# One step less in the head and one more in the tail of a long LSTM, with the head's vector and scalar work put in another order

## The chip, the cores and the metric

One NeuronCore of a Trainium2 chip runs the whole kernel. The metric is the device time of one execution in microseconds (us), as the median over runs. Everything is float32.

## The reference

The input `x` is 32 sequences of 512 steps with 512 features. The output is `x` plus the hidden states of an LSTM that runs over it:

```python
xW = einsum('ntd,dg->ntg', x, Wx) + b          # 512 -> 4*512 gates
def step((h, c), xw_t):
    a = xw_t + h @ Wh                          # Wh: 512 x 2048
    i, f, o = sigmoid(a[:, :1536]) in thirds;  g = tanh(a[:, 1536:])
    c = f * c + i * g
    h = o * tanh(c)
out = x + (all h)                              # h starts as cond_1024, c as 0
```

The 512 steps must run one after another; `xW` needs no `h` and may be made ahead.

## The kernel before

**Plain and grouped steps.** The product `x_t @ Wx` is made in two ways. A *plain* step multiplies one step's 32 rows by all of Wx (`plain_block` in the head, `plain_part` in the tail). A *group* takes 32 steps at once (GS) as a matrix product cut in 4 x 2 x 4 blocks, which a fast scheme makes with 26 block products instead of 32 (R = 26); each of them is again made by 7 products instead of 8 (`ROW`, r = 1 to 7). The price is additions on VectorE: *U sums* of x blocks (`U_SUMS`, `make_sum`, called through `u_ahead`), *V sums* of weight blocks (`V_SUMS`, `v_sum`, once, in the head, then stored to DRAM in `vdram` and loaded row by row into `vring`), and *W sums* of finished products (`W_SUMS`, `W_OF`, `w_op`), whose results go to DRAM (`xwd`) and come back as one tile `xw` for each step (`load_xw`). In front of the U sums stand `pair_sum`s of the x blocks.

512 steps = 20 plain ones at the start (HEAD), 15 groups of 32, and 12 plain ones at the end (TAIL).

**The stream.** TensorE's matmuls of the groups form one list (`items`), emitted in *units* of which four make one of the 7 products of a block product (a *slot*). A group has 26 x 7 x 4 = 728 units. `emit_matmuls(n)` emits n units; `evacuate()` copies or adds finished results out of PSUM (ScalarE copies L643, L652, L659; VectorE adds L649, L653, L656) into buffers `cbuf`, and hands buffers out of the list `free_c`. Some slots begin from a bias difference that is copied into their bank before the first product (`seed_banks`, L620; which one by `BIAS_OF`; the differences are made by `early_seeds`, `second_seeds` and `late_seeds`).

**One step t** is: `h_part(t)`, 16 matmuls of h by Wh into the bank that already holds xW (L270); then stream units, or plain pieces (L198), in which TensorE is busy while `cell(t)` runs on ScalarE (L285 to L287, L292) and VectorE (L289 to L296) and leaves the transposed h for the next `h_part`. Every engine runs its instructions in the order in which the program lists them, so what stands in front of `cell(t)` on ScalarE or VectorE delays it.

**The head, t < 20.** Steps 0 to 4 have two plain steps each beside the `h_part` (`HEAD_PLAINS`: at t = 2 the plain steps 18 and 19) and jobs on VectorE: V sums, pair sums, the first U sums (`jobs`). Steps 5 to 19 run the first group's 728 units by `HEAD_STREAM`, steps 6 to 9 with one plain step more each in pieces. Plain results for t >= 14 are parked in DRAM (`kept`). From t = 5 on a step's units are cut in chunks: the first has 24 units (16 at t = 5) and `cell(t)` stands right behind it; each later chunk (12 units) begins with `evacuate`, pair sums, U sums for 24 units ahead and W sums, as many as a budget of VectorE time (`room["dve"]`) allows.

**The middle, 20 <= t < 468 (END),** has one `h_part` and 22 or 24 units in each step, the units one group ahead of the steps that use them.

**The tail.** When the stream ends, xW of the last 12 steps is made in 192 pieces of 128 columns (`plain_tail`): 11 at t = 468, 13 at t = 469, then five in each step (`due`). From t = 470 (SPLIT) on a step's bank is split in two halves with a cell each. The weights for the pieces are loaded again, since their buffers were used otherwise: one entry of `late_loads` at each t in `LATE` = (453, 455, 457, 463, 465, 467, 468); the last two (`last_load`, L229) bring the rows for c = 2 and c = 3. The rows of x for t = 500 to 503 are loaded at t = 457 into one half of `seeds_own` (`x_early`).

Of the kernel before, what the change touches and what calls it, by code (L numbers as in the profile page):

```python
# [12 lines left out]
P = 128  # L13
B = 32
T = 512
NJ = 4
G = 4
TC = 8
NCHUNK = T // TC
H = P // 2  # L20
W = G * P
HW = G * H

HEAD = 20
GS = 32
NG = 15
TAIL = T - HEAD - NG * GS
# [7 lines left out]
PARKED = 14  # L35
# [4 lines left out]
SPLIT = END + 2  # L40
LATE = (453, 455, 457, 463, 465, 467, 468)

FIRST = 13
HEAD_PLAINS = ((14, 15), (16, 17), (18, 19), (5, 6), (11, 12), (), (7,), (8,), (9,), (10,))
HEAD_STREAM = (0, 0, 0, 0, 0, 24, 52, 48, 56, 56, 56, 56, 56, 56, 56, 56, 48, 44, 36, 28)
HELD = 4
# [59 lines left out]
def kernel(  # L106
# [63 lines left out]
    def x_of(t):  # L170
        return xnat[:, xslot(t // TC), t % TC]

    x_early = seeds_own[:, 0].rearrange("p (t q b) -> p t q b", t=TC // 2, q=NJ)

    def x_plain(t):
        if 2 * TC <= t < HEAD:
            return xnat[:, 2, t % TC]
        return x_early[:, t % 4] if T - 12 <= t < T - TC else x_of(t)

# [51 lines left out]
    late_loads = [late_load(0, 0, 4), late_load(1, 0, 4)]  # L231
    late_loads += [lambda: nc.sync.dma_start(out=seeds_own[:, 0], in_=x[NCHUNK - 2][:, TC // 2 * P : TC * P])]
    late_loads += [late_load(2, 4, 6), late_load(3, 4, 6), lambda: last_load(2), lambda: last_load(3)]
# [22 lines left out]
    def half_of(t, i):  # L256
        if is_split(t):
            return PAIRS[t % 2][i][:, 0:HW]
        return bank_of(t)[:, i * HW : (i + 1) * HW]
# [61 lines left out]
    last_x = []  # L321
    free_u = [0, 1, 2, 3, 4, 5]
    room = {"dve": 0.0}
# [304 lines left out]
    def u_ahead(n):  # L628

        last = min((pos[0] + n - 1) // 4, len(items) - 1)  # L630
        if last >= 0:
            make_u(max(items[i][1] for i in range(max(0, last - 7), last + 1)))
# [171 lines left out]
    def flush_v():  # L804
        for f in v_stores:
            f()
        v_stores.clear()
# [11 lines left out]
    def split_seeds(of):  # L819
        for i in of:  # L820
            sub(seed_rows[i][:, HW:W], seed_rows[i][:, HW:W], seed_rows[i][:, 0:HW])
# [12 lines left out]
    def late_seeds():  # L834
        q = seed_rows
        split_seeds((1, 2))
        sub(q[3], q[1], q[4])
        sub(q[3], q[3], q[0])
        sub(q[1], q[1], q[2])
        seeds_made.extend(("b0-b3", "b3", "b0-b1+b2"))  # L840

# [26 lines left out]
    with tc.manual_schedule():  # L868
# [52 lines left out]
        jobs[2] = sums(21, 22, 23)  # L921
        jobs[3] = [lambda: pair_sum(0, (0, 1))] * 4 + [lambda: u_ahead(8)] + sums(24)
        jobs[4] = sums(25) + [lambda: u_ahead(24), early_seeds]
        raws = lambda *ids: [lambda s=s: v_raw(s) for s in ids]
        jobs[5] = raws(0, 7, 17, 24)
        jobs[6] = raws(1, 8, 15, 21)
        jobs[7] = raws(2, 3)
        jobs[8] = [second_seeds]
        jobs[10] = [late_seeds]
        ends = {  # L930
# [18 lines left out]
        for t in range(T):  # L949
# [25 lines left out]
            if t == 7:  # L975
                load_seeds(((0, 2),))
            if t + 2 == HEAD:
                load_xw(t + 2)
            if PARKED <= t + 3 < HEAD + NG * GS and t + 3 != HEAD:
                load_xw(t + 3)  # L980

            if t < HEAD_STEPS:
# [3 lines left out]
                if t > 4:  # L986
                    chunks.append(("stream", {5: 16}.get(t, 24), None))
                    left -= chunks[0][1]
                pieces = [(k, p, cs) for k, p in plain for cs in (((0, 1, 2, 3),) if t < 5 else ((0,), (1,), (2,), (3,)))]
# [11 lines left out]
                for i, (kind, m, cs) in enumerate(chunks):  # L1001
# [16 lines left out]
                    else:  # L1018
# [5 lines left out]
                        evacuate()  # L1024
                        if i == 0:
                            while wqueue and (room["dve"] > 2200 or len(free_c) < 1):
                                w_op(len(free_c) < 1)
                        else:
                            row_jobs(4)
                            u_ahead(m + 24)  # L1030
                            while wqueue and (
                                room["dve"] > (-2500 if t >= 13 and any(row_of(v[1]) == 0 for v in wqueue) else 800)
                                or len(free_c) < 2
                            ):
                                w_op(len(free_c) < 2)
                        seed_banks(m)
                        if i == 0 and t + 1 in SEEDED and t + 1 < HEAD:
                            seed_step(t + 1)
                        emit_matmuls(m)
                        room["dve"] += m * PROD / 4  # L1040
                        if i == 0:
                            cell(t)
                            if t + 1 == HEAD:
                                seed_step(t + 1)
                            room["dve"] -= 2500.0
                            while todo and not plains:
                                todo.pop(0)()
                                flush_v()
                if t >= 5:
                    load_v_ahead()  # L1050
# [11 lines left out]
            if t == HEAD_STEPS:  # L1062
                room["dve"] = max(room["dve"], -1500.0)
            wait_at_end[0] = t >= END - 2
# [86 lines left out]
```

## Time and profile before

| | before |
|---|---|
| median of 3 runs | 3091.01 us (3089.55 to 3091.67) |
| the profiled execution | 3091.39 us, span 3089.6 us |
| TensorE (PE) busy | 3064.1 us, 99% of the span |
| VectorE (DVE) busy | 2350.0 us, 76% |
| ScalarE (ACT) busy | 1473.4 us, 48% |
| GpSimd (POOL) busy | 240.4 us, 8% |
| mean granted TensorE clock | 0.999 |

PE is TensorE's matmul row, SP the queue that issues the DMAs. The span is from the first to the last instruction; 1.8 us of the execution lie around it. A line number such as L270 is a line of the kernel. The ends of matmuls are modelled: where they follow each other without a break, the start of the next one is the better mark.

### The profile page before, as it was taken

The page shows a single profiled execution, that of the slowest core. Times are in us where ns is not written, and L with a number is a line of the kernel's source. Part 1 is how long each engine was busy: PE and PEld are TensorE (multiplying, and loading weights), DVE is VectorE, ACT ScalarE, POOL GpSimd, SP SyncE. Part 2 cuts the span into 40 slices and gives each one's busy share as a digit, 9 for nine tenths or more (in the row PEclk, how much of TensorE's full clock was granted, in tenths as well). Part 3 has the DMA queues.
Part 4 walks back from the last instruction along what each step waited for, and adds up shares of the span by engine and source line. Part 5 has one row for each costly group of instructions (what it writes and reads, how often), then busy time and mean ns, then how long its engine had stood idle before and what let it go on. Part 6 is the DMA issues. An engine that isn't in the chain of part 4 may idle for free.

```text
span 3089.6 us, 108356 instructions
## 1 busy us (share of the span) xinstructions
PE 3064.1 (99%) x43600; PEld 1659.5 (54%) x43600; DVE 2350.0 (76%) x6382; ACT 1473.4 (48%) x5528; POOL 240.4 (8%) x508
## 2 busy tenths in 40 slices
PE   9899999999999999999999999999999999999998
PEld 7655555555555555555555555555555555555675
DVE  7678787787777878778787787878778787787644
ACT  2344544445454444545445454454544545444444
POOL 0000000000000000000000000000000000000110
PEclk9999999999999999999999999999999999999999
DMA  9788878787777777778778787877878777887530
GB/s 337 253 263 267 279 248 272 237 264 238 247 260 249 254 241 254 256 239 272 234 258 263 226 270 242 259 249 241 268 241 264 238 247 260 250 261 260 176 92 22
DMA packets 318454, 753.26 MB, mean 244 GB/s; under 512 B 50816, under 2 KB 101504, under 8 KB 317440
## 3 DMA queue, kind: packets, MB, share of 16 engines
q1 hardware_dynamic: 317952, 746.33, 74.3%
q8 instruction: 344, 5.64, 0.8%
q14 instruction: 158, 1.29, 0.1%
HBM read 564.46 MB, written 184.81 MB: 243 GB/s over the span
## 4 chain that ended last, share of the span: by engine, by line
PE 95%; DVE 2%; DMA 1%; ACT 0%; issue 0%; SPq 0%; DVEq 0%; ACTq 0%
PE gbank L270 53%; PE xbank L577 32%; PE bbank L577 5%; PE xbank L270 2%; PE xbank L207 1%; DMA vdram<-ubuf 0%; PE gbank L198 0%; DMA r<-in_L_cond_b_dram 0%; DVE prod L289 0%; DVE s L290 0%; DMA vdram<-xs 0%; DVE ubuf L771 0%; DMA xw<-kept 0%; DVE ht L296 0%; DVE hbuf L294 0%
## 5 line engine op out<-in xcount | busy, mean ns | idle before, releaser
L270 PE MATMUL gbank<-wh_sb,ht 128*32 128x512 f32 (+1 forms) x16288 | 1778.7, 575 | 6.1 <-DVE ht L296 4.4
L270 PEld LDWEIGHTS gbank<-wh_sb,ht 128*32 128x32 f32 x16288 | 607.7, 110 | 831.3 <-issue 702.9
L577 PE MATMUL xbank<-vring,ubuf 128*32 128x256 f32 (+1 forms) x13584 | 853.1, 369 | 5.5 <-ACT cbuf L659 2.3
L285 ACT ACTIVATE s<-gbank 128x128 f32<-128x128 f32 x976 | 274.0, 281 | 1213.2 <-PE gbank L270 1212.6
L577 PEld LDWEIGHTS xbank<-vring,ubuf 128*32 128x32 f32 x13584 | 527.7, 110 | 296.5 <-issue 135.1
L289 DVE TENSOR_TENSOR prod<-s 128x128 f32<-128x128 f32 x1024 | 293.4, 286 | 489.0 <-ACT s L286 484.6
L304 POOL TENSOR_TENSOR oc<-xnat,ht 128x128 f32<-128x128 f32 x504 | 240.2, 477 | 2811.4 <-DVE ht L296 1335.6
L292 ACT ACTIVATE tanh_c<-s 128x64 f32<-128x64 f32 x1024 | 262.4, 256 | 255.0 <-DVE s L290 252.3
L296 DVE STREAM_TRANSPOSE ht<-hbuf 128x64 f32<-128x64 f32 x1022 | 250.8, 245 | 75.8 <-DVE hbuf L294 1.6
L730 ACT COPY gbank<-xw 128x512 f32<-128x512 f32 x459 | 276.0, 601 | 3.7 <-DMA xw<-xwd 3.5
L290 DVE TENSOR_TENSOR s<-prod 128x64 f32<-128x64 f32 x1024 | 230.3, 225 | 35.2
L294 DVE TENSOR_TENSOR hbuf<-o,tanh_c 128x64 f32<-128x64 f32 x1024 | 211.3, 206 | 31.2 <-ACT tanh_c L292 30.7
L286 ACT ACTIVATE s<-gbank 128x64 f32<-128x64 f32 x976 | 226.0, 232 | 0.0
L437 DVE TENSOR_TENSOR cbuf<-cbuf 128x1024 f32<-128x1024 f32 x181 | 219.3, 1217 | 1.1
L577 PE MATMUL xbank<-vring,r 128*32 128x256 f32 (+1 forms) x3216 | 208.3, 357 | 0.0
L577 PE MATMUL xbank<-vring,xs 128*32 128x256 f32 (+1 forms) x3120 | 203.9, 358 | 0.0
L577 PE MATMUL bbank<-vring,ubuf 128*32 128x256 f32 (+1 forms) x2600 | 185.3, 343 | 3.8 <-DVE cbuf L649 3.8
L577 PEld LDWEIGHTS xbank<-vring,r 128*32 128x32 f32 x3216 | 123.1, 110 | 78.6 <-issue 45.7
L287 ACT ACTIVATE o<-gbank 128x128 f32<-128x128 f32 (+1 forms) x509 | 155.5, 305 | 0.0
L577 PEld LDWEIGHTS xbank<-vring,xs 128*32 128x32 f32 x3120 | 120.9, 111 | 59.0 <-issue 24.0
L643 ACT COPY cbuf<-xbank 128x512 f32<-128x512 f32 x222 | 129.5, 583 | 29.1 <-PE xbank L577 20.6
L577 PEld LDWEIGHTS bbank<-vring,ubuf 128*32 128x32 f32 x2600 | 101.3, 110 | 73.1 <-issue 41.0
(162 smaller groups left out, 2509.0 us busy)
## 6 DMA issues: line engine op xcount, KB each, us to landing
vring<-vdram SPq DMA_DIRECT2D x310, 896.0 KB, 5.7
xw<-xwd SPq DMA_DIRECT2D x1920, 64.0 KB, 4.3
xwd<-cbuf SPq DMA_DIRECT2D x135, 512.0 KB, 4.4
xwd<-r SPq DMA_DIRECT2D x85, 512.0 KB, 4.8
out_dram<-oc SPq DMA_DIRECT2D x255, 128.0 KB, 4.2
xnat<-in_x_dram SPq DMA_DIRECT2D x62, 512.0 KB, 6.4
xs<-in_x_grouped_dram SPq DMA_DIRECT2D x45, 512.0 KB, 4.7
vring<-vdram SPq DMA_DIRECT2D x33, 512.0 KB, 4.9
```

Source lines behind the costliest of these rows:

```text
L270: nc.tensor.matmul(dst[j * B : (j + 1) * B], state["ht"][:, k], m, start=False, stop=True, skip_group_check=True)
L285: nc.scalar.activation(s[:, u, 0:2], g[:, n_, 0:2], AF.Sigmoid)
L286: nc.scalar.activation(s[:, u, 2], g[:, n_, 3], AF.Tanh)
L289: nc.vector.tensor_mul(prod[:, u], s[:, u, 0:2], s[:, u, 2:4])
L290: add(nxt[:, u, 3], prod[:, u, 0], prod[:, u, 1])
L292: nc.scalar.activation(tanh_c[:, HALVES[u]], nxt[:, u, 3], AF.Tanh)
L294: nc.vector.tensor_mul(hbuf[:, HALVES[u]], o[:, u], tanh_c[:, HALVES[u]])
L296: nc.vector.transpose(ht[:, 2 * u : 2 * u + 2].rearrange("p q b -> p (q b)"), hbuf[:, HALVES[u]])
L304: (nc.gpsimd if t < T - 8 else nc.vector).tensor_add(oc[:, tt % 2], x_of(t), ht)
L437: op(c_of(dst), c_of(src), c_of(bb))
L577: nc.tensor.matmul(dst[j * B : (j + 1) * B, cols], left_of(gr, s, r)[:, j * B : (j + 1) * B], right_of(row, slot, RIGHT[r])[:, cols], star ...
L730: nc.scalar.copy(bank_of(t), src)
```

## The change

HEAD becomes 19 and TAIL 13: step 2 loses the plain step 19, and the head's last step goes. The 728 units of the first group then lie in steps 5 to 18, 60 of them in steps 10 to 14. In steps from t = 10 with at least 48 units (t = 10 to 16) the first chunk is cut to 12 units and `cell(t)` moves behind the second chunk of 24, and so behind that chunk's `evacuate` and `seed_banks`. The five operations of `late_seeds` become three jobs that are spread over the later chunks of step 10. In later chunks W sums come first and then U sums for 44 units ahead if more than three U buffers are free; the first U sums (`u_ahead(8)`) move from step 3 to step 4, behind V sum 24, and take other buffers (`free_u`); another `u_ahead(40)` is added at step 5. In the first group, the first `xw` tile of each eight steps is loaded two steps ahead instead of three. At the end of the head the VectorE budget may start at -2600 ns instead of -1500. With 13 tail steps END becomes 467 and SPLIT 469, while `LATE` stays; `x_early` holds a whole chunk of x in both halves of `seeds_own`.

```diff
-HEAD = 20
+HEAD = 19
...
-HEAD_PLAINS = ((14, 15), (16, 17), (18, 19), (5, 6), (11, 12), (), (7,), (8,), (9,), (10,))
-HEAD_STREAM = (0, 0, 0, 0, 0, 24, 52, 48, 56, 56, 56, 56, 56, 56, 56, 56, 48, 44, 36, 28)
+HEAD_PLAINS = ((14, 15), (16, 17), (18,), (5, 6), (11, 12), (), (7,), (8,), (9,), (10,))
+HEAD_STREAM = (0, 0, 0, 0, 0, 24, 52, 52, 56, 56, 60, 60, 60, 60, 60, 56, 52, 44, 36)
...
-    x_early = seeds_own[:, 0].rearrange("p (t q b) -> p t q b", t=TC // 2, q=NJ)
+    x_early = seeds_own.rearrange("p s c -> p (s c)").rearrange("p (t q b) -> p t q b", t=TC, q=NJ)
...
-        return x_early[:, t % 4] if T - 12 <= t < T - TC else x_of(t)
+        return x_early[:, t % TC] if T - TAIL <= t < T - TC else x_of(t)
...
-    late_loads += [lambda: nc.sync.dma_start(out=seeds_own[:, 0], in_=x[NCHUNK - 2][:, TC // 2 * P : TC * P])]
+    late_loads += [lambda: nc.sync.dma_start(out=seeds_own.rearrange("p s c -> p (s c)"), in_=x[NCHUNK - 2])]
...
-            return PAIRS[t % 2][i][:, 0:HW]
+            return PAIRS[(t - SPLIT) % 2][i][:, 0:HW]
...
-    free_u = [0, 1, 2, 3, 4, 5]
+    free_u = [2, 3, 0, 1, 4, 5]
...
     def late_seeds():
         q = seed_rows
-        split_seeds((1, 2))
-        sub(q[3], q[1], q[4])
-        sub(q[3], q[3], q[0])
-        sub(q[1], q[1], q[2])
-        seeds_made.extend(("b0-b3", "b3", "b0-b1+b2"))
+        return [
+            lambda: split_seeds((1, 2)),
+            lambda: (sub(q[3], q[1], q[4]), sub(q[3], q[3], q[0])),
+            lambda: (sub(q[1], q[1], q[2]), seeds_made.extend(("b0-b3", "b3", "b0-b1+b2"))),
+        ]
...
-        jobs[3] = [lambda: pair_sum(0, (0, 1))] * 4 + [lambda: u_ahead(8)] + sums(24)
-        jobs[4] = sums(25) + [lambda: u_ahead(24), early_seeds]
+        jobs[3] = [lambda: pair_sum(0, (0, 1))] * 4 + sums(24)
+        jobs[4] = [lambda: u_ahead(8)] + sums(25) + [early_seeds, lambda: u_ahead(24)]
...
-        jobs[5] = raws(0, 7, 17, 24)
+        jobs[5] = [lambda: u_ahead(40)] + raws(0, 7, 17, 24)
...
-        jobs[10] = [late_seeds]
+        jobs[10] = late_seeds()
...
-            if t + 2 == HEAD:
-                load_xw(t + 2)
-            if PARKED <= t + 3 < HEAD + NG * GS and t + 3 != HEAD:
-                load_xw(t + 3)
+            for d in (2, 3):
+                first_rows = HEAD <= t + d < HEAD + GS and (t + d - HEAD) % TC == 0
+                if PARKED <= t + d < HEAD + NG * GS and (d == 2) == first_rows:
+                    load_xw(t + d)
...
                 if t > 4:
-                    chunks.append(("stream", {5: 16}.get(t, 24), None))
-                    left -= chunks[0][1]
+                    late_cell = t >= 10 and left >= 48
+                    for m in (12, 24) if late_cell else (16 if t == 5 else 24,):
+                        chunks.append(("stream", m, None))
+                        left -= m
+                else:
+                    late_cell = False
...
                         evacuate()
-                        if i == 0:
+                        if i <= late_cell:
                             while wqueue and (room["dve"] > 2200 or len(free_c) < 1):
                                 w_op(len(free_c) < 1)
                         else:
...
                                 w_op(len(free_c) < 2)
+                            if len(free_u) > 3:
+                                u_ahead(m + 44)
                         seed_banks(m)
-                        if i == 0 and t + 1 in SEEDED and t + 1 < HEAD:
+                        if i == 0 and t + 1 in SEEDED and t + 1 != HEAD:
                             seed_step(t + 1)
                         emit_matmuls(m)
                         room["dve"] += m * PROD / 4
-                        if i == 0:
+                        if i == late_cell:
                             cell(t)
...
-                            while todo and not plains:
+                            while todo and not plains and t < 10:
                                 todo.pop(0)()
                                 flush_v()
+                        elif i > late_cell and not plains:
+                            for _ in range(-(-len(todo) // (len(chunks) - i))):
+                                todo.pop(0)()
...
-                room["dve"] = max(room["dve"], -1500.0)
+                room["dve"] = max(room["dve"], -2600.0)
```

## The prediction

> **What bounds the kernel now.** I read the page first, then the table of windows over single steps, then TensorE's waits, and then the timelines of VectorE and ScalarE at each wait.
>
> ```profile
> PE 3064.1 (99%) x43600; PEld 1659.5 (54%) x43600; DVE 2350.0 (76%) x6382; ACT 1473.4 (48%) x5528; POOL 240.4 (8%) x508
> ```
>
> TensorE is busy for 99% of the span. The change keeps its work: as many `h_part`s, 32 plain steps, 728 units per group. So it can only act on the other 1%, and on time at a lower clock. The windows (sum of each engine, then granted clock, DMA share, GB/s) show where these lie: step 10, steps 10 to 19, step 13, and everything from t = 468.
>
> ```profile
> 142.72:159.05 16.33, 12.52 (x151) 6.99 (x144) 10.02 (x25) 5.77 (x18) 0.46 (x1) 0.79 0.93 329
> 142.72:241.93 99.21, 91.47 (x1311) 48.73 (x1305) 75.38 (x176) 43.66 (x141) 4.82 (x9) 0.97 0.83 273
> 179.78:189.26 9.48, 9.48 (x149) 5.60 (x144) 6.66 (x17) 4.31 (x15) 0.46 (x1) 1.00 0.80 254
> 2883.59:3089.60 206.01, 195.78 (x3675) 133.64 (x3672) 101.77 (x385) 93.19 (x437) 21.90 (x37) 0.99 0.26 77
> ```
>
> TensorE's own waits (us in total, times, longest) name what it stands for:
>
> ```profile
> PE gbank L270 <- DVE ht L296: 4.4, 5, 1.2
> PE bbank L577 <- DVE cbuf L649: 3.8, 1, 3.8
> ...
> PE xbank L577 <- ACT cbuf L659: 2.3, 3, 0.9
> PE xbank L577 <- issue: 1.7, 1, 1.7
> ...
> PE gbank L270 <- DVE hbuf L294: 1.5, 1, 1.5
> PE xbank L577 <- DVE ubuf L491: 1.3, 1, 1.3
> ```
>
> **The price of a clean step.** Step 13 has 56 units and no idle time: 9.48 us. In it the first unit follows 3.44 us after its `h_part` began:
>
> ```profile
> 183.22 0.64 PE L577 MATMUL bbank<-vring,ubuf 128*32 128x256 f32 x8
> ```
>
> So `h_part` costs 3.44 and a unit (9.48 - 3.44) / 56 = 0.108 us.
>
> **Steps 10 to 19** hold ten `h_part`s and 492 units: 34.4 + 53.1 = 87.5 us clean, against 99.21. They lose 11.7. More than half of that is step 10, 6.85 over the clean 9.48:
>
> ```profile
> 149.87 0.43 DVE L821 TENSOR_TENSOR cbuf<-cbuf 128x256 f32<-128x256 f32 x1 [1.11 <-DMA cbuf<-in_L_cond_b_dram]
> ...
> 153.25 1.08 PE L577 MATMUL bbank<-vring,ubuf 128*32 128x256 f32 x8 [3.81 <-DVE cbuf L649]
> ```
>
> `late_seeds`, right behind `cell(10)`, waits until 149.87 for a DMA and then runs five operations, while the result that the next product needs (L649) stands behind it. Then the clock halves: at a mean of 0.79 over 16.33 us it was at half for 16.33 x 0.21 x 2 = 6.9 us, so from about 152.1, 2.7 us after TensorE had stopped; until 159.05 it cost half of 5.8 us. The change splits the five operations over the end of step 10, behind results that TensorE awaits; the loads are issued at the end of step 9 as now and should land 7.2 us into step 10 as now (149.87 - 142.72), before the third chunk ends (3.44 + 48 x 0.108 = 8.6). The differences are first needed for slot 12 at step 11, with a whole `h_part` for cover. I count all 6.85 as gone; without cover it is the 3.81.
>
> The rest, 4.8 us, are waits at the start of a later chunk, as here:
>
> ```profile
> 166.07 1.08 DVE L491 TENSOR_TENSOR ubuf<-ubuf 128x896 f32<-128x896 f32 x1
> ...
> 167.25 2.37 PE L577 MATMUL xbank<-vring,ubuf 128*32 128x256 f32 x40 [0.71 <-ACT cbuf L659]
> ```
>
> The view names L659, but slot 13's first product needs neither that copy nor its bank; it reads the U sum that ends at 167.15, queued behind the cell. The 1.7 at step 18 is also two U sums. Looking 44 units ahead, and having U sums of the second chunk ahead of the cell, takes these away.
>
> **Steps 4, 6 and 20.** At step 4 the cell stands behind a U sum that waits 5.16 us for a store out of its buffer; with the new buffer order and place it finds a buffer stored earlier, and the cell is early: -1.2 (the longest wait of `h_part` above). At step 6 the U sum of slot 3 comes at step 5: -1.3. Step 20 waits 1.5 for a cell behind three W sums and four pair sums; a budget of 3800 - 2600 = 1200 leaves room for one W sum at most: -1.5.
>
> ```profile
> 76.81 1.09 DVE L491 TENSOR_TENSOR ubuf<-xs 128x896 f32<-128x896 f32 x1 [5.16 <-DMA vdram<-ubuf]
> ```
>
> The waits of 0.8 at step 5 and 0.9 at step 7 stay: step 5 is cut as before, and at step 7 three free U buffers are left, not more than three, so slot 5's sum comes as late as now.
>
> **The step that moves.** The head loses one `h_part` and one plain step, 3.44 + 3.46 (60.44 - 56.98 below). In the tail the chain of waits shows a step with five pieces (36.87 to 41.40) and one without (54.66 to 59.13):
>
> ```profile
> 3036.87 3.45 PE gbank L270 x64
> 3040.32 1.08 PE xbank L207 x24
> 3041.40 3.45 PE xbank L270 x64
> ...
> 3054.66 2.40 PE gbank L270 x40
> ...
> 3059.13 2.42 PE xbank L270 x40
> ```
>
> Pieces fill time in which TensorE waits for the split cell: 4.53 with, 4.47 without. Of 192 pieces 24 are done at t = 468 and 469; the other 168 fill 33 split steps with five and one with three, and eight have none. After, it is 208 - 24 = 184: 36 with five, one with four, six with none: 3 x 4.53 - 2 x 4.47 = +4.65. Net of the move: -2.25.
>
> **What is late next, at step 2.** Without plain step 19, TensorE is free at 56.98. But `cell(2)` stands on VectorE behind four V sums, the last of which waits for a store, and the first half of h is there at 59.35:
>
> ```profile
> 56.98 3.72 PE L198 MATMUL xbank<-r,xnat 128*32 128x256 f32 x64
> 60.44 1.12 PE L270 MATMUL xbank<-wh_sb,ht 128*32 128x512 f32 x8
> ```
> ```profile
> 55.76 0.96 DVE L771 TENSOR_TENSOR xs<-r,vring 128x768 f32<-128x768 f32 x1 [1.86 <-DMA vdram<-xs]
> ...
> 59.11 0.24 DVE L296 STREAM_TRANSPOSE ht<-hbuf 128x64 f32<-128x64 f32 x1
> ```
>
> Nothing ahead of it changes, so 2.4 of the 3.46 come back: +2.4 (0.5 if that DMA wait went).
>
> **What is late next, in the tail.** END moves by a step, `LATE` does not. Before, the rows for c = 3 are issued during t = 468:
>
> ```profile
> L229 SPq DMA_DIRECT2D cbuf<-in_L_cond_Wx_dram x4: 422/426/432, 2880.3 to 2887.2; - x4
> ...
> DMA to landing us min/median/max: 4.1/4.2/4.8
> ```
>
> The last of them starts at 2887.2, 3.6 us after `h_part(468)` (2883.59), and lands 4.2 later, at 7.8. Their first use is in step 469 now. After the change, step 468 is the second step with pieces: pieces 11 to 23 of the list (counted from 0), c = 3 from piece 20, so at 3.44 + 9 x 3.46 / 16 = 5.4 us after `h_part(468)`. SP has the same queue ahead (the store of t = 467, four loads of `xw`). TensorE waits 7.8 - 5.4 = +2.4 (0 if SP gets there two microseconds sooner).
>
> **The new order in steps 10 to 16.** Now 12 units, a chunk's copies, and only then the cell. In step 13 the last half of h was done at 185.79, 2.57 after `h_part`:
>
> ```profile
> 185.54 0.25 DVE L296 STREAM_TRANSPOSE ht<-hbuf 128x64 f32<-128x64 f32 x1
> ```
> ```profile
> 143.41 0.58 ACT L643 COPY cbuf<-xbank 128x512 f32<-128x512 f32 x1 [3.28 <-DMA xwd<-cbuf]
> ```
>
> With 12 units (1.30) and about two copies (0.58 each by L643) ahead it is done 5.0 after, while TensorE has 52 to 60 units, 5.6 to 6.5 us: covered, with 0.6 to 1.5 to spare. Copies behind the cell then come only just before the third chunk needs them. No row shows this order. Nearest are the 0.7 waits, of which steps 10 to 19 have about one every second step; nine steps with nothing are 0, nine with 0.8 each 7.2. I take 3.
>
> **The sum:** -11.7 - 1.2 - 1.3 - 1.5 - 2.25 + 2.4 + 2.4 + 3.0 = -10.2. Four more units at step 7 are paid by later steps (728 in all). The profiled execution took 3091.39, 0.4 above the median, so about 3081 on the median's scale. About 0.2%, 6.2 us, is what a measurement of this kernel can tell from no change: 3084.8 to 3097.2.
>
> **Rivals.**
>
> *VectorE becomes the head's bound* (14%). Steps 10 to 18 are 9 x 3.44 + 488 x 0.108 = 83.7 us clean.
>
> ```profile
> L289 DVE TENSOR_TENSOR prod<-s 128x128 f32<-128x128 f32 x20 | 5.7, 287 | 13.4 <-ACT s L286 13.4
> ```
>
> The row groups the first operation of the cell's halves in the old ten steps: VectorE idles 13.4 us ahead of them. It works 75.38 us there, 73.5 without one cell (1.9 by the busy time of L289 to L296), which leaves 10.2 of 83.7. Nine tenths of 13.4 is 12.1: the head would be 1.9 us longer than clean by these waits alone. If nine tenths of all idle time stay, 0.9 x (99.21 - 75.38) = 21.4, it is 11.2 longer. Between them, at 8 instead of 3, stands this rival: 3086. Against it: W sums for rows needed later may move behind the head, where VectorE is less full (76% of the span).
>
> *The two new gaps halve the clock* (7%). Step 10 shows a drop about 2.7 us into a gap, and the new ones are 2.4. Each drop costs 2.9: 3081 + 5.8 = 3086.8. The Trainium skill (TensorE: Matmul & The Clock Gate, "Why this matters for your kernels") warns of gaps above about 3 us; by that rule neither gap is long enough, and the trace agrees in so far as the 1.7 gap brought no drop and the 3.8 one did.
>
> *Slower: a copy ahead of the cell waits for a buffer* (7%). The L643 row above shows the wait, 3.28 for a store out of `cbuf`, at a place where no cell stood behind it. In the new order one does: a wait of 3.28 uses up the 1.5 to spare, and a longer one makes a gap like step 10's, 6.85 with the clock. Shorter steps press on the buffers. Against 10.2 gained, two such gaps give 3094.7 and three 3101.6; from three of the seven steps on it is slower.
>
> **How the numbers follow.** 72% for the forecast, 3081. The rivals of 14% and 7% end within 0.2%, the last is slower. Faster by over 0.2%: 0.73 (with a little of the first rival's low end); within: 0.20; slower: 0.07. Low end: no new waits in steps 10 to 18 (-3), half of the two other gaps (-2.4), some of the two old waits: 3075. High end, with the first two rivals in it: 3089.
>
> **What would show it.** TensorE's waits should have no L649 of 3.8, no half clock before the kernel's end, and two new entries: `h_part(3)` for 2.4 on h, and L207 for 2 on the DMA of L229. The step from `h_part(10)` should take about 9.9. Steps 10 to 18 above 90 us, or a clock below 1 in them, would show me wrong; so would ScalarE waits on `xwd` ahead of L285.

## The result: slower by 0.4%

| | before | after |
|---|---|---|
| median | 3090.98 us (3089.55 to 3091.67, 7 runs) | 3102.95 us (3098.30 to 3107.99, 7 runs) |
| the profiled execution | 3091.39 us, span 3089.6 us | 3102.61 us, span 3100.8 us |

The ratio is 1.0038, with a 95% interval of 1.0028 to 1.0047: slower by about 12 us. 3081 was forecast, 3075 to 3089.

The page of the changed kernel has TensorE 4.0 us busier and the span 11.2 us longer:

```profile
PE 3068.1 (99%) x43640; PEld 1659.9 (54%) x43640; DVE 2351.3 (76%) x6383; ACT 1471.2 (47%) x5528; POOL 241.8 (8%) x508
```

The windows that answer to those of before: step 10, steps 10 to 18, step 13, then steps 19 to 23, and everything from t = 467.

```profile
138.62:148.53 9.91, 9.91 (x158) 7.76 (x152) 5.16 (x19) 5.07 (x16) 0.46 (x1) 1.00 0.97 336
138.62:234.27 95.65, 85.21 (x1271) 48.46 (x1265) 73.09 (x170) 41.68 (x133) 6.20 (x9) 1.00 0.75 257
171.40:184.51 13.11, 10.29 (x157) 4.89 (x153) 9.49 (x20) 4.87 (x16) 0.45 (x1) 1.00 0.97 331
234.27:273.36 39.09, 33.04 (x404) 15.58 (x400) 26.20 (x65) 14.45 (x54) 1.83 (x4) 0.91 0.86 266
2884.20:3100.80 216.60, 205.17 (x3808) 150.15 (x3808) 104.41 (x394) 95.16 (x447) 22.34 (x38) 0.99 0.26 76
```

Step 10 became clean, 9.91 us with no idle time and a full clock. But steps 10 to 18 take 95.65, 12.0 over the clean 83.7: by the starts of their `h_part`s, 2.9 are lost at step 11, 6.1 in steps 12 to 16 and 3.0 at step 18. In step 13, which lost nothing before, TensorE now stands for 2.8. The next five steps have 22, 22, 24, 22 and 22 units, in a clean state 4 x 5.81 + 6.02 = 29.26 (the step times before); they take 39.1. In the kernel before, the five steps behind the head took 31.0, at nearly the same DMA share and GB/s, so it is not that more bytes are moved there now:

```profile
241.93:272.93 31.00, 29.47 (x405) 15.13 (x401) 27.19 (x68) 14.55 (x55) 2.30 (x5) 1.00 0.84 261
```

TensorE's waits have new names:

```profile
PE gbank L270 <- DVE hbuf L294: 6.3, 3, 3.9
PE xbank L577 <- ACT xbank L620: 4.1, 2, 2.6
PE xbank L270 <- DVE ht L296: 3.7, 4, 1.4
PE xbank L577 <- DMA vring<-vdram: 2.8, 1, 2.8
PE xbank L207 <- DMA r<-in_L_cond_Wx_dram: 1.9, 1, 1.9
...
PE xbank L577 <- ACT xnat L659: 1.3, 1, 1.3
PE bbank L577 <- DVE r L649: 1.3, 1, 1.3
PE xbank L207 <- DMA cbuf<-in_L_cond_Wx_dram: 1.2, 1, 1.2
```

Four places stand behind most of them, each with rows of the changed kernel's timelines.

**Step 11.** The last of the bias differences (L839) ends at 154.1; it was queued behind four pair sums, a U sum and a W sum, and ScalarE's copy of it (L620) holds TensorE for 2.6:

```profile
153.43 0.68 DVE L839 TENSOR_TENSOR cbuf<-cbuf,r 128x512 f32<-128x512 f32 x1
...
154.20 1.11 ACT L620 COPY xbank<-cbuf 128x512 f32<-128x512 f32 x2 [5.00 <-DVE cbuf L839]
...
154.84 0.42 PE L577 MATMUL xbank<-vring,ubuf 128*32 128x256 f32 x4 [2.62 <-ACT xbank L620]
```

**Step 13.** The cell stands behind the evacuation of the second chunk and a W sum (177.02 to 178.15). What the next chunk needs (L649) stands behind the cell, and the chunk after it waits for L620, which ScalarE runs only after it has copied products that this first wait made late. TensorE waits twice:

```profile
177.02 1.22 DVE L437 TENSOR_TENSOR cbuf<-cbuf,r 128x1024 f32<-128x1024 f32 x1
178.15 0.28 DVE L289 TENSOR_TENSOR prod<-s 128x128 f32<-128x128 f32 x1
...
180.22 0.39 DVE L649 TENSOR_TENSOR r<-bbank,r 128x256 f32<-128x256 f32 x1
...
180.67 0.64 PE L577 MATMUL bbank<-vring,ubuf 128*32 128x256 f32 x8 [1.34 <-DVE r L649]
183.22 1.07 PE L577 MATMUL xbank<-vring,ubuf 128*32 128x256 f32 x16 [1.48 <-ACT xbank L620]
```

**Steps 17 to 22.** SP spends 7.1 us on the first eight loads of `xw`: eight issues, and waits for the store of W sums just before (221.22) and for earlier transfers. Behind them stand weights, for which TensorE waits 2.85 at step 18, and the x row that the pair sums of step 18 need: VectorE waits 5.4, these four sums and three W sums stand in front of `cell(19)`, and `h_part(20)` waits 3.9. Three steps later ScalarE's copy ahead of the cell waits for a store out of its buffer, and `h_part(23)` waits 2.1.

```profile
221.22 0.38 SPq L454 DMA_DIRECT2D xwd<-r  x1
221.66 0.57 SPq L672 DMA_DIRECT2D vdram<-in_L_cond_Wx_dram  x1
222.33 7.11 SPq L719 DMA_DIRECT2D xw<-xwd  x8
229.54 0.84 SPq L695 DMA_DIRECT2D vring<-vdram  x2
230.44 0.63 SPq L512 DMA_DIRECT2D xs<-in_x_grouped_dram  x1
...
233.41 1.07 PE L577 MATMUL xbank<-vring,xs 128*32 128x256 f32 x16 [2.85 <-DMA vring<-vdram]
...
237.58 0.42 DVE L522 TENSOR_TENSOR xs<-xs 128x256 f32<-128x256 f32 x1 [5.35 <-DMA xs<-in_x_grouped_dram]
...
244.22 2.56 PE L270 MATMUL gbank<-wh_sb,ht 128*32 128x512 f32 x16 [3.93 <-DVE hbuf L294]
...
260.53 0.58 ACT L643 COPY r<-xbank 128x512 f32<-128x512 f32 x1 [3.06 <-DMA xwd<-r]
...
265.88 4.43 PE L270 MATMUL gbank<-wh_sb,ht 128*32 128x512 f32 x24 [2.12 <-DVE hbuf L294]
```

**The tail.** Two waits for the rows of L229, 1.9 and 1.2, and half clock behind them.

### The profile page after: what moved, and what is told of

Same layout as the page of the kernel before. It is cut to its first block, busy times and chain, and to the rows that moved or that the text cites. A ratio compares the mean times of both kernels' runs of the same rounds, so it can differ in the third digit from the quotient of the medians.

```text
span 3100.8 us, 108464 instructions
## 1 busy us (share of the span) xinstructions
PE 3068.1 (99%) x43640; PEld 1659.9 (54%) x43640; DVE 2351.3 (76%) x6383; ACT 1471.2 (47%) x5528; POOL 241.8 (8%) x508
## 4 chain that ended last, share of the span: by engine, by line
PE 95%; DVE 1%; DMA 1%; ACT 0%; issue 0%; SPq 0%; DVEq 0%; ACTq 0%
PE gbank L270 53%; PE xbank L577 32%; PE bbank L577 5%; PE xbank L270 3%; PE xbank L207 1%; PE gbank L198 1%; DMA xwd<-r 0%; DMA vring<-vdram 0%; DMA xs<-in_x_grouped_dram 0%; DVE prod L289 0%; DMA vdram<-xs 0%; DVE s L290 0%; DMA cbuf<-in_L_cond_Wx_dram 0%; DVE hbuf L294 0%; DVE ht L296 0%
## 5 line engine op out<-in xcount | busy, mean ns | idle before, releaser
L437 DVE TENSOR_TENSOR cbuf<-cbuf 128x1024 f32<-128x1024 f32 x164 | 198.7, 1217 | 0.8
```

Of the source, the lines that this page charges most:

```text
L437: op(c_of(dst), c_of(src), c_of(bb))
```

## The experiments

Times are medians beside runs of the kernel before on the same chip; the ratio is to those, with its 95% interval. The first four experiments shared a chip, and so did e5 to e8, e9 to e12, f1 to f4, and f5 and f6; the kernel before had medians of 3090.0 to 3091.3 there, so differences of 1 us between chips tell nothing. The table gives for every profile the start of `h_part(10)`, of the first step after the head and of the fifth after that, and what lies between over the clean 83.7 (head of 19) or 87.5 (head of 20), and over 29.26. A profile is one execution: up to step 11 several of these programs are the same, and there they differ by up to 4 us. Most profiles lie within 2.2 us of their run's median, but those of e3 (3095.32) and f3 (3094.59) are of the slowest execution, 5.8 and 4.3 above it.

| run | median us | starts | steps 10 to 18 or 19 lose | next five lose |
|---|---|---|---|---|
| before | 3090.98 | 142.72, 241.93, 272.93 | 11.7 | 1.7 |
| after | 3102.95 | 138.62, 234.27, 273.36 | 12.0 | 9.8 |
| e1_late | 3097.95 | 138.68, 236.40, 275.10 | 14.0 | 9.4 |
| e2_cell | 3102.41 | 140.82, 234.69, 271.19 | 10.2 | 7.2 |
| e3_order20 | 3089.55 | 139.42, 234.47, 267.83 | 7.5 | 4.1 |
| e4_split19 | 3104.19 | 143.00, 238.78, 273.88 | 12.1 | 5.8 |
| e5_seeds | 3090.20 | 143.02, 240.40, 271.41 | 9.9 | 1.7 |
| e6_pool | 3101.48 | 138.78, 234.48, 272.92 | 12.0 | 9.2 |
| e7_row | 3103.17 | 138.86, 235.09, 269.99 | 12.5 | 5.6 |
| e8_half | 3104.71 | 138.60, 235.08, 273.63 | 12.8 | 9.3 |
| e9_store | 3099.09 | 141.52, 239.21, 271.13 | 14.0 | 2.7 |
| e10_both | 3103.79 | 137.94, 238.70, 272.36 | 17.1 | 4.4 |
| e11_order20_store | 3093.57 | 140.17, 237.32, 273.48 | 9.6 | 6.9 |
| e12_before_store | 3097.88 | 142.20, 244.84, 278.68 | 15.1 | 4.6 |
| f1_raw19 | 3104.73 | 139.08, 239.80, 273.07 | 17.0 | 4.0 |
| f2_raw20 | 3086.81 | 140.16, 235.29, 267.11 | 7.6 | 2.6 |
| f3_mend19 | 3090.31 | 140.83, 232.98, 270.62 | 8.4 | 8.4 |
| f4_mend20 | 3083.47 | 140.12, 233.65, 263.75 | 6.0 | 0.8 |
| f5_first20 | 3083.86 | 139.37, 233.37, 263.12 | 6.5 | 0.5 |
| f6_first19 | 3103.21 | 138.53, 236.50, 275.27 | 14.3 | 9.5 |

**The tail alone (e1_late).**

```diff
-LATE = (453, 455, 457, 463, 465, 467, 468)
+LATE = (452, 454, 456, 462, 464, 466, 467)
```

> The kernel after, with the seven steps of LATE each one earlier, so that they stand to END as before. Theory: the changed kernel loses 3.1 us in the tail (L207 waits 1.9 for the rows of L229 and 1.2 for a copy behind them) and 1.7 more in a half-clock window there; both go, so 4.8 below the changed kernel, about 3098 against 3103, and steps up to 466 as they are. Rival: the loads one step earlier meet the buffers' last users or SP's queue and wait, or the gap only moves to another piece: within 1 us of the changed kernel.

3097.95 us, ratio 1.0023 (1.0013 to 1.0032): 5.0 below the changed kernel. L207 is gone from the waits, and the tail, the row below, is 4.6 longer than before (206.01), which is the forecast price of the moved step:

```profile
2885.50:3096.10 210.60, 202.29 (x3808) 132.07 (x3808) 104.41 (x394) 95.17 (x447) 22.42 (x38) 1.00 0.26 78
```

**The place of the cell (e2_cell).**

```diff
-                    late_cell = t >= 10 and left >= 48
+                    late_cell = False
```

> The kernel after, with the cell of steps 10 to 16 again directly behind the first chunk of 24 units. Theory (VectorE's other work, not the place of the cell, makes the head late): of the 12.0 us that steps 10 to 18 lose, only the waits on a copy or sum whose queue held the cell go (3.2 at step 13, 1.5 at step 15, 0.9 at step 16), and some 0.7 waits at later chunks come back for them: about 3 below the changed kernel, 3100; the 2.6 at step 11 and what steps 19 to 23 lose (9.8) stay. Rival (the late cell is the cause): steps 10 to 18 come down to about 87 us, and the kernel to about 3094 or less.

3102.41, 1.0035 (1.0021 to 1.0048). The sum hardly moved, but the stages did. Steps 12 to 16 took 49.95 us, and 54.37 in the changed kernel (first the run, then the changed kernel):

```profile
166.87:216.82 49.95, 48.70 (x740) 28.24 (x736) 39.85 (x91) 24.28 (x76) 3.00 (x5) 1.00 0.80 264
```
```profile
161.34:215.71 54.37, 49.40 (x740) 26.81 (x736) 40.49 (x94) 23.51 (x76) 4.37 (x5) 1.00 0.74 249
```

Steps 10 and 11 lost 3.3 for it (26.05 against 22.72): behind a first chunk of 24 the four pair sums of step 10 come a chunk sooner and wait for their x row. They, a U sum and the first job of `late_seeds` stand in front of the L649 that TensorE needs:

```profile
150.03 0.43 DVE L522 TENSOR_TENSOR r<-r 128x256 f32<-128x256 f32 x1 [1.75 <-DMA r<-in_x_grouped_dram]
```
```profile
153.77 0.64 PE L577 MATMUL bbank<-vring,ubuf 128*32 128x256 f32 x8 [3.65 <-DVE cbuf L649]
```

So the late cell helps in step 10 and harms from step 12 on.

**Order alone and cut alone (e3_order20, e4_split19).**

```diff
-HEAD = 19
+HEAD = 20
...
-HEAD_PLAINS = ((14, 15), (16, 17), (18,), (5, 6), (11, 12), (), (7,), (8,), (9,), (10,))
-HEAD_STREAM = (0, 0, 0, 0, 0, 24, 52, 52, 56, 56, 60, 60, 60, 60, 60, 56, 52, 44, 36)
+HEAD_PLAINS = ((14, 15), (16, 17), (18, 19), (5, 6), (11, 12), (), (7,), (8,), (9,), (10,))
+HEAD_STREAM = (0, 0, 0, 0, 0, 24, 52, 48, 56, 56, 56, 56, 56, 56, 56, 56, 48, 44, 36, 28)
```

This is e3 against the kernel after; e4 is the kernel before with the opposite of it (and the lines of `x_early` and `PAIRS`).

> The new order of the head with the old cut: 20 steps in the head with the old list of units and plain steps, 12 in the tail. Theory (the new order gains in step 10, but makes SP's queue and the copies late between steps 10 and 23 whatever the cut): the 13.3 us of the old head's losses (11.7 in steps 10 to 19, 1.6 elsewhere) go, some 10 to 15 come back, and the tail is as in the kernel before: 3088 to 3093. Rival (it is the cut: the same VectorE work in a head shorter by a step): with 20 steps the order alone gains what was forecast for it, 3091 - 14 + 3 = about 3080.

> The new cut with the old order: 19 steps in the head with the new list of units, 13 in the tail, everything else as before. Theory (order, not cut): it keeps the old head's losses and takes the net of the move (-2.25), 1.4 at step 2, and 4.8 in the tail: 3091 + 4 = about 3095. Rival (the cut): the head is then short of VectorE time whatever the order, W sums are late for the stores of the first rows, and the time is 3103 or more.

The order alone: 3089.55, 0.9996 (0.9987 to 1.0004), no difference. The cut alone: 3104.19, 1.0042 (1.0029 to 1.0055), as slow as both together. My theory expected 3095 there: it is the cut that costs, with either order (some 13 us, of which e1 finds 5 in the late rows of the tail). The order brings the start of step 20 forward by 7.5 us (234.47 for 241.93), but the five steps behind the head then lose 4.1 for 1.7, and by step 29 the profile is 0.7 ahead (295.88 for 296.60). It ends 3.6 behind; being the slowest of its 11 executions it overstates what the order gives back.

**The differences alone (e5_seeds)**, in the kernel before; the diff is that of `late_seeds` and of the two places that run `todo`.

> The kernel before with one part of the change: the five operations of late_seeds as three jobs over the later chunks of step 10. Theory of the prediction (step 10 loses 6.85, three idle and three by the clock, and the differences have a whole h_part for cover): 3091 - 6.85 = about 3084. Rival (the last difference is made at step 11 behind other VectorE work, and the bank's copy waits for it there; what the head gains is also given back by step 28): step 10 falls to about 9.5 but step 11 rises by 2 to 4, and the total is 3088 to 3091.

3090.20, 0.9997 (0.9988 to 1.0005). Step 10 fell from 16.3 to 10.8, and step 11 rose from 10.4 to 14.0: the rival.

**What is short behind the head (e6 to e8).** One takes the first eight loads off SP, one moves the late x row ahead of them, one makes the W sums of the first group over half of their columns and leaves the other half out:

```diff
+            queue = nc.gpsimd if t < HEAD + 2 else nc.sync
+            queue.dma_start(out=dst[j * B : (j + 1) * B], in_=xwd[g % 2][m, q * B : (q + 1) * B, j])
```
```diff
-... for p, q in ((-10, 0), (-9.5, 1), (-2.5, 2), (3.5, 3))]
+... for p, q in ((-10, 0), (-9.5, 1), (-3.5 if g == 1 else -2.5, 2), (3.5, 3))]
```
```diff
+        cut = 512 if gr.g == 0 else 1024
+        op(c_of(dst)[:, 0:cut], c_of(src)[:, 0:cut], c_of(bb)[:, 0:cut])
```

> The kernel after, with the loads of the first two grouped rows (xw for t = 19 and 20, eight transfers at step 17) issued by GpSimd instead of SP. Theory (SP's queue stands 7.1 us at those loads until a late store has landed, and the weights for step 18 and the x blocks for the pair sums of step 18 stand behind them): the 2.9 at step 18 and most of the 3.9 and 1.7 at step 19 go, 5 to 8 below the changed kernel: 3095 to 3098. Rival (VectorE's arrears of W sums are the limit, SP only shows them): TensorE waits as long one or two steps later, and the time is within 1.5 us of 3103.

> The kernel after, with the load of the next group's third x row issued one row of units earlier (at step 16, ahead of the loads of xw on SP). Theory of SP's queue: the pair sums at 237 no longer wait 5.4 us, the cell behind them is early, and the 3.9 before the next h_part and its half-clock window (1.7) go; the 2.9 at step 18 for weights stays: about 5 below the changed kernel, 3098. Rival (VectorE's arrears): 3102 to 3104.

> The kernel after, with each W sum of the first group made over half of its columns (512 of 1024), so that some 80 operations of 1.22 us take about 0.65; nothing else is left out, the order and all waits are as they are. Theory of VectorE's arrears: the waits in steps 12 to 16 and 19 to 23 go, and TensorE gains 12 to 20 us: 3083 to 3091. Rival (SP's queue and single misplaced operations, VectorE has time enough): less than 5 us, 3098 or more.

3101.48 (1.0035, 1.0021 to 1.0048), 3103.17 (1.0035, 1.0022 to 1.0047) and 3104.71 (1.0040, 1.0027 to 1.0052): three misses of the theories. The last is the clearest. With W sums of 0.68 us instead of 1.22 nothing is gained, so the time of these sums is not the limit. Its profile shows one thing that is: two W sums end by 251.8, SP issues their stores only at 258.4, behind weights and loads of `xw`, and the copy into that buffer waits until 261.4, with the cell behind it:

```profile
250.52 0.68 DVE L438 TENSOR_TENSOR r<-cbuf,r 128x512 f32<-128x512 f32 x1
251.12 0.69 DVE L438 TENSOR_TENSOR cbuf<-cbuf,r 128x512 f32<-128x512 f32 x1
```
```profile
256.41 1.92 SPq L720 DMA_DIRECT2D xw<-xwd  x4
258.43 0.39 SPq L455 DMA_DIRECT2D xwd<-r  x1
258.92 0.41 SPq L455 DMA_DIRECT2D xwd<-cbuf  x1
```
```profile
261.43 0.59 ACT L644 COPY r<-xbank 128x512 f32<-128x512 f32 x1 [6.62 <-DMA xwd<-r]
```

**The stores in another queue (e9 to e12).**

```diff
-            nc.sync.dma_start(
+            (nc.sync if gr.g else nc.gpsimd).dma_start(
                 out=xwd[gr.g % 2][2 * tau : 2 * tau + 2, :, j].rearrange("m p c -> p m c"),
```

e10 has the first group's loads of `xw` there too, e11 is e3 with the stores moved, e12 the kernel before with the stores moved.

> The kernel after, with the W sums' stores of the first group (xwd, L454) issued by GpSimd instead of SP. In the kernel with half W sums two such sums ended at 251.8 and SP issued their stores only at 258.4, behind weights that wait for TensorE, an output store and eight loads of xw; ScalarE's copy ahead of the cell waited for the landing until 261.4. Theory of SP's order (buffers come back late because stores stand in one queue with loads that wait): the losses of steps 18 to 23 (12.9 in the changed kernel) shrink to 3 to 5, and the time is 3094 to 3097. Rival (the stores' landing itself, or the scarce buffers whatever the queue): copies still wait, 3101 to 3104. Second rival (GpSimd's own queue: its additions stand behind the stores' waits, and the output stores on SP behind them): new waits of SP on GpSimd, 3103 or more.

> As the run before, and the loads of xw for the first group's 32 steps on GpSimd too. Theory of SP's order: a little better than the stores alone, since the first loads no longer stop SP for 7 us at step 17: 3091 to 3095. Rival (with the first loads GpSimd issued late and h_part waited 2.7 for xw): loads stand behind stores that wait for VectorE, and several steps wait for xw by 1 to 3 us each: 3100 or more.

> The new order with the old cut (20 and 12) and the first group's W stores on GpSimd. By the theory of SP's order the order alone reached step 20 7.5 us ahead of the kernel before and gave it back by step 29, at copies that waited for stores; with the stores in another queue at least half of that stays: 3082 to 3086. Rival (buffers, whatever the queue): 3088 to 3092 as without.

> The kernel before with only the first group's W stores on GpSimd. Its head has no TensorE wait on a store and one of 1.5 at step 20, so both theories expect little: 3089 to 3091.5. If GpSimd's queue does harm by itself it shows here as more than 3093.

e9: 3099.09, 1.0026 (1.0015 to 1.0037), above the theory's 3094 to 3097. The five steps behind the head lose 2.7 instead of 9.8, at a full clock; but step 10 takes 14.5, since the copy there now waits for a store that landed 9.5 us after GpSimd issued it (138.91 to 148.36; the same store on SP in the changed kernel took 5.2, 135.47 to 140.66):

```profile
141.52:155.99 14.47, 11.88 (x159) 6.50 (x152) 6.26 (x20) 5.00 (x16) 1.10 (x2) 0.88 0.83 316
...
239.21:271.13 31.92, 29.67 (x404) 15.10 (x400) 26.19 (x65) 14.42 (x54) 4.71 (x8) 1.00 0.94 311
```
```profile
148.46 0.59 ACT L643 COPY cbuf<-xbank 128x512 f32<-128x512 f32 x1 [10.83 <-DMA xwd<-cbuf]
```

e10 3103.79 (1.0044, 1.0032 to 1.0056), e11 3093.57 (1.0007, 0.9998 to 1.0016), e12 3097.88 (1.0023, 1.0014 to 1.0031): with its stores on GpSimd the kernel before takes 7 us more, 3.4 of them in step 10 and 2.9 in the five steps behind the head. So which queue issues the stores matters, and GpSimd's is no better place for all of them. That the stores alone decide the five steps is not shown: in e9 these start 4.9 later than in the changed kernel (239.21 for 234.27), so SP had more time to catch up, and step 24 comes only 2.2 sooner. e7, which moves one x row on SP and starts them 0.8 later, has step 24 sooner by 3.4.

**Fewer transfers behind the head, and the mends together (f1 to f4).**

```diff
-            if HEAD - 2 <= t < HEAD - 2 + 3 * len(V_DIRECT):
-                s, d = divmod(t - HEAD + 2, 3)
-                store_raw(V_DIRECT[s], d)
+            if HEAD + 12 <= t < HEAD + 12 + 3 * len(V_DIRECT):
+                s, d = divmod(t - HEAD - 12, 3)
+                store_raw((24, *V_DIRECT)[s], d)
...
-                    late_cell = t >= 10 and left >= 48
+                    late_cell = 10 <= t < 12
```

f1 is the kernel after with the first part, f2 e3 with it; f3 is f1 with the second part and e1's `LATE`, f4 f2 with the second part.

> The kernel after, with the 24 transfers of raw weight blocks to DRAM (L672, one in each of the steps 17 to 40) moved to steps 31 to 54, where fewer transfers are made; the blocks are read from step 47 on. Theory of transfers in flight (10.2 transfers a step in steps 19 to 23, 6.6 of at most 8 in flight): one in ten less there gives back 3 to 6 of the 12.7 lost in steps 18 to 23: 3097 to 3100. Rival (single places: the 7.1 us at step 17 and the burst behind it): these stay, 3101 to 3104.

> The new order with the old cut, and the same 24 transfers moved by 14 steps. Theory of transfers in flight: most of what was gained by step 20 (7.5) and given back by step 29 stays: 3083 to 3086. Rival: given back as before, 3088 to 3091.

> The kernel after with three mends: LATE a step earlier, the raw transfers 14 steps later, and the cell behind the second chunk at steps 10 and 11 alone (from step 12 on behind the first chunk of 24, as before). With the cell early, steps 12 to 16 took 4.4 us less in the trace of that run, and with it late, steps 10 and 11 took 3.3 less. If the causes add: 3103 - 5 - 4.4 - 3 to 6 = 3088 to 3091. Rival (what the head gains is given back in steps 19 to 43 whatever it is): 3096 to 3098, as with LATE alone.

> The new order with the old cut, the raw transfers 14 steps later and the late cell at steps 10 and 11 alone. If the causes add: 1 to 3 below the same without the last, 3081 to 3085. Rival (given back): 3088 to 3091.

f1: 3104.73, 1.0049 (1.0036 to 1.0063), a miss: its profile loses 4.0 in the five steps, but step 11 took 16.4 there, the five steps began 5.5 later, and step 24 came only 0.3 sooner. f2: 3086.81, 0.9989 (0.9980 to 0.9998), between the theory's range and the rival's; against the kernel before on its own chip it is 1.5 better than e3, and the intervals overlap. f3: 3090.31, 1.0001 (0.9992 to 1.0009), 7.6 below e1 (6.4 when each is set against the kernel before on its chip). f4: 3083.47, 0.9979 (0.9969 to 0.9988), faster than both kernels: the new order, the old cut, the late cell at steps 10 and 11 alone and the raw transfers later. Its windows from step 10 to 19, 20 to 24 and 25 to 28 have the clock at 1.00 throughout:

```profile
140.12:233.65 93.53, 88.55 (x1311) 51.91 (x1305) 74.78 (x176) 43.47 (x141) 4.82 (x9) 1.00 0.87 289
233.65:263.75 30.10, 29.47 (x405) 15.14 (x401) 25.99 (x67) 14.58 (x55) 2.29 (x5) 1.00 0.76 239
263.75:287.42 23.67, 23.67 (x333) 12.43 (x333) 20.16 (x54) 10.97 (x43) 1.84 (x4) 1.00 0.90 275
```

**The needed difference first (f5_first20, f6_first19):** f4 and the kernel after with the second and third job of `late_seeds` exchanged, for one operation more.

```diff
-            lambda: (sub(q[3], q[1], q[4]), sub(q[3], q[3], q[0])),
-            lambda: (sub(q[1], q[1], q[2]), seeds_made.extend(("b0-b3", "b3", "b0-b1+b2"))),
+            lambda: (sub(q[1], q[1], q[2]), seeds_made.extend(("b0-b3", "b3"))),
+            lambda: (add(q[3], q[1], q[2]), sub(q[3], q[3], q[4]), sub(q[3], q[3], q[0]), seeds_made.append("b0-b1+b2")),
```

> The new order with the old cut, the raw transfers 14 steps later and the late cell at steps 10 and 11 alone, as before, and in late_seeds the difference that slot 12 needs made right after the two splits, the one for slot 19 behind it in the third job (one operation more). In that kernel's profile ScalarE's bias copies at step 11 hold TensorE 1.9 and 1.5 us. Theory (the difference comes late because it is the last operation, behind pair sums, a U sum and a W sum): 2 to 4 below it, 3079.5 to 3081.5. Rival (the pair sums, which wait for their x blocks, hold all three jobs alike): 3083 to 3084.

> The kernel after with only that reordering of late_seeds. Theory: the 2.6 at step 11 and the half clock that follows it in some runs go, 2.5 to 5 below the changed kernel, 3098 to 3100.5, and the runs spread less. Rival: the third gap is filled by the next wait, or given back by step 23: 3102 to 3104.

3083.86 (0.9976, 0.9967 to 0.9986) and 3103.21 (1.0041, 1.0027 to 1.0055): the time that the rivals gave, both times. But in the traces the needed difference was not held alike. In f6 ScalarE's copy of it holds TensorE for 1.25 instead of 2.62, and in f5 not at all instead of for 1.9. Other waits came in its place (for weights, and at later chunks), and step 11 took 13.7 and 13.8, where it took 12.8 and 13.3.

## Why the prediction was wrong

On the profile's scale 3081.2 was forecast and 3102.6 came, 21.4 more. Set against the terms of the working, 6.0 more were lost in steps 10 to 16, 3.0 at step 18, 9.6 in steps 19 to 23 and 3.6 in the tail, and 1.0 less at step 2: together 21.2.

- **"The new order in steps 10 to 16", +3.0.** These steps lose 9.0, above even the term's upper bound of 7.2: 2.9 at step 11, which is the next point, and 6.1 in steps 12 to 16. I had bounded the term by 0.7 waits of the old order, in which no cell stands behind a second chunk's copies. The cell itself was covered, as forecast; what I put off with one clause, that copies behind the cell come "only just" in time, is what failed (2.8 at step 13), and I had counted only copies ahead of the cell, where in step 13 a W sum of 1.1 stands too. e2's trace prices the place of the cell at 4.4 in steps 12 to 16; f4 against f2 confirms it in the time, 3.3.
- **"A whole `h_part` for cover" of `late_seeds`.** 6.85 at step 10 went, but 2.6 came back at step 11 here, and step 11 of e5 rose by 3.7. Five profiles whose program is the same up to there took 12.8 to 16.4 us for step 11. The cover was counted from the end of step 10, while three VectorE jobs of that step run into step 11. f5 and f6 show that this wait is not all that holds step 11: with it shorter the step was not.
- **"Step 20", -1.5.** The budget left the step one W sum, as meant, but the four pair sums of the step before it, which waited 5.4 for their x row, and two W sums behind them ran late and stood in front of the cell as well. The steps 19 to 23 lose 9.8 where I left 0.2: 9.6 more; and step 18 lost 3.0 for weights behind the same loads. I asked of each moved step what its queue carries, but not of SP what a head shorter by a step leaves it to issue there. e8 rules out the time of the W sums; the rows of steps 17 to 22 and e7, with 4.2 less in steps 19 to 23 for one x row issued sooner, point to SP's order; but of the runs that eased it alone only e9 shortened the time, by some 4 us with intervals that overlap, so this cause is argued more than shown. e4 shows that the cut costs as much with the old order.
- **The net of the move, -2.25.** Even with the tail, the cell and the raw transfers mended, a head of 19 takes 6.8 us more than a head of 20 (f3 and f4), where the working had -2.25, and +2.4 for the wait at step 2. Which wait takes the rest was not settled.
- **The tail, +2.4.** +4.65 for the moved step was right (4.6 in e1). The late rows cost 3.1 instead of 2.4, and the clock, which the term left out, and what follows 2.9 more: 6.0 in the traces, 5.0 in the time.
- **Right:** step 10 at 9.9 us without half clock; steps 4 and 6; step 2, where `h_part(3)` waits 1.4 instead of 2.4; and 0.6 and 0.9 at steps 5 and 7 stayed.

Of the rivals, VectorE as the bound finds no support in e8. That gaps like these halve the clock was right in kind (three windows in the profile, 1.7 each). The copy that waits for a buffer ahead of a cell did happen, at step 22 instead of 10 to 16, where I had looked for it.

**Open:** in the kernels with a head of 19 the two losses of the table add up to 17 to 24, and single mends that took 2 to 6 out of one stage (e2, e7, f1) did not move the time; only f3, with two beside `LATE`, did. In these kernels step 19 starts anywhere from 233.0 to 239.8, but step 24 only from 270.0 to 275.3: those that come late to the five steps (from 238.7 on) lose 2.7 to 5.8 in them, the others 5.6 to 9.8. What couples the stages so was not settled. Fewer transfers was my last explanation: on average 6.6 of SP's transfers were in flight in steps 19 to 23 and 4.9 in steps 60 to 100, worked out from their starts and landings; none starts before the eighth before it has landed. The kernel before has 6.2 in its five steps behind the head and loses only 1.7 there, and f1, with fewer transfers, has 6.5: so this explanation is not borne out, and f2's gain is too small to carry it.

## What to carry to other kernels

A step saved on the busiest engine can be lost again where the queues feed the next stage: list for each in-order queue, the DMA issuer too, what it must issue in the shortened stage, and which buffer comes back only when a store behind those loads has landed. An operation that is moved has to be costed for what then stands behind it, not only for whether it is itself on time. A shortened stage and a new order are best measured apart: here one change held both, and hid that the order could help.

## What the hardware showed

The clock is decided in windows of 3.41 us that do not start with a gap. The half-clock stretches of the changed kernel are each 3.41 us long and start at whole multiples of 3.41 from each other (245.37, 265.85 and 2900.94). Eight of these windows, in four pairs: two pairs across a long gap, and two with a gap in the first window:

```profile
149.81:153.22 3.41, 2.41 (x24) 0.82 (x16) 3.38 (x7) 0.00 (x0) 0.00 (x0) 1.00 1.02 427
153.22:156.63 3.41, 1.78 (x36) 1.10 (x40) 3.41 (x6) 2.22 (x5) 0.00 (x0) 1.00 0.47 188
228.31:231.72 3.41, 2.25 (x44) 1.29 (x35) 2.15 (x10) 2.35 (x8) 0.45 (x1) 1.00 0.41 107
231.72:235.13 3.41, 1.72 (x25) 0.97 (x29) 0.51 (x2) 0.60 (x2) 0.00 (x0) 1.00 0.95 319
241.96:245.37 3.41, 1.15 (x12) 0.50 (x16) 3.20 (x13) 1.64 (x5) 0.46 (x1) 1.00 0.90 271
245.37:248.78 3.41, 3.41 (x20) 1.08 (x16) 2.19 (x3) 0.00 (x0) 0.00 (x0) 0.50 0.98 283
262.43:265.85 3.42, 1.34 (x31) 0.79 (x20) 3.24 (x9) 1.00 (x6) 0.00 (x0) 1.00 1.03 320
265.85:269.26 3.41, 3.38 (x16) 0.92 (x20) 3.34 (x5) 1.50 (x3) 0.46 (x1) 0.50 0.98 266
```

TensorE's gaps of 2.6 (152.22 to 154.84) and 2.9 (230.56 to 233.41) fall on two windows each, no window has less than 1.72 us of work, and the clock stays. The gap of 2.1 before 265.88 lies in one window, which is left with 1.34, and the next runs at half clock. Laid over all 20 profiles, each on the phase of its own half-clock stretches, the same grid divides the windows at full clock (from 26 us on, the last two of each profile left out) without an exception: the 47 that hold up to 1.45 us of matmul time, by its modelled ends, are followed by half clock, and the some 17,800 that hold 1.46 or more are not. So here it took about 2 us of idle time in one window, not a gap of some length. The Trainium skill (TensorE: Matmul & The Clock Gate, "What's actually happening") states such a free-running window of 3413 ns, and the trace agrees; its rule of gaps above about 3 us ("Why this matters for your kernels"), by which I priced the rival, does not hold for this 2.1 us gap. That a gap's place in the window decides would also explain a part of the spread of the changed kernel's runs; their mean clocks, 0.999 in the fastest (3098.30) and 0.997 in the slowest (3107.99), fit that.
